# Separate PSUM tiles for a convolution's two halves, sums written straight to the gates, and later loads in a graph-network kernel

## The chip, the cores and the metric

The kernel runs on one core of a Trainium2 chip, in fp32. The time is that of the device in microseconds (us), from the start to the end of one execution. One execution was also recorded by the hardware profiler, and its trace is what the lines below come from.

A core has five engines with a queue each: PE (TensorE, the matrix products), ACT (ScalarE), DVE (VectorE), POOL (GpSimd) and SP (SyncE, which here only issues DMA transfers). Products go to PSUM, [...]a bank holds 512 fp32 values in each of 128 partitions.

## The reference, cut to what matters

One layer of a graph network over 32 graphs (batches) of 512 nodes with 256 features. `h` is the input after a layer norm and a ReLU.

```
h  = relu(layernorm(x))
hc = transpose(h)                                   # features x nodes
c  = relu(bn1(conv1x1(hc)));  c = bn2(conv17(c))    # 17 taps along the nodes
x_conv = transpose(relu(c + hc))
s  = h @ w_se.T + b_se                              # 3 values for a node
A  = exp(-|s_n - s_m|^2) * adj                      # 512 x 512
x_nmp  = A @ relu(h @ w_msg.T + b_msg)
gi = concat(x_conv, x_nmp) @ w_ih.T + b_ih;  gh = h @ w_hh.T + b_hh
r, z = sigmoid(gi_r + gh_r), sigmoid(gi_z + gh_z)
out  = x + (1 - z) * tanh(gi_n + r * gh_n) + z * h
```

The convolution with 17 taps (256 to 256 channels), the messages with their gathering, and the gates are nearly all of the products.

## The kernel before

Features lie on the 128 partitions in two halves (ND = 2), the 512 nodes of a batch along the free axis. Every batch passes through five kinds of work:

- **begin**: norm, ReLU and transpose of a batch to `hT`, which is stored to DRAM (`hd`) by POOL's queue. Three users load it back with SP: `load_row` (`hT`, for the first convolution), `load_graph` (`hTg`, for messages) and `load_gates` (`hTb`, for gates).
- **rows**: the 1x1 convolution, whose rows are the input of the long one.
- **conv**: the 17 taps as a fast convolution with 5 x 5 = 25 products. It doesn't go by batches: the nodes are cut in units of 18 rows, 29 units a batch, and the units lie in seven groups (`STARTS`). The first group has 116 units, which is four batches; the other six have some 135. A group runs its 25 products (`convolution`, L741). Each has transformed weights `w`, an operand `x` made by DVE ahead of time and, except one product of the 25 (`LONE`), a sum operand `xd`. From the second group on, a product writes both output halves into one PSUM tile `pair` of two banks (L777). Half 0 is started by four small products with `w[:, 2]`, ACT copies it into half 1, and the `xd` products are then added to both (L817 to 822). ACT then hands the finished pair over to SBUF (`both`, L620) as `n` or `z`, and DVE adds up the results of the 25 products in `y` (`summed`).
- **graph**: messages, the factors, `kernel_exp` (L878) with four products of 5 rows that run beside each other, one of which goes to the second bank of `pair` (L885) and three to banks of the pool `ps_g`; ACT takes the exponential into `at`. Then come the mask (`masked`, L897), the gathering (`gather`), and the store of `xnb` to DRAM (`nd`).
- **gates**: products with `whh` and `wih` into `ps_acc`, tanh on ACT, mixing on DVE, and the output, with `load_res` (L934) fetching the input block by block.

Between conv and gates stands `evacuate` (L679). When a group's `y` is complete, there is a list `EVAC` with an entry for each batch and half. ACT applies the batch norm to each and writes a `part`, a buffer of three, POOL stores it to DRAM (`cd`), and when all of a batch is there, `load_conv` loads it as `xconv`. `residual` (L234) adds `hTb` on DVE and takes ReLU on ACT.

The order is made by a planner that writes out every instruction beforehand. Five streams (rows, begins, graphs, conv, gates; L1308 to 1314) are Python generators with a clock of progress each; the planner takes the stream that is furthest behind and not waiting, and keeps an estimate `now` of the time on PE and of when DVE and ACT come free (`dve.free`, `act.free`). Work for DVE and ACT that isn't tied to a stream is put in between by `fill` (L1259), which runs delayed actions (`later`), evacuations and background work. An evacuation is given out only if ACT is estimated to be free soon:

```
if now < t or act.free > now + 0.3 or len(PARTS) > 2 and now < PARTS[-3]:
    return False
```

So an edit to an estimate, to a wait or to a `later` moves the order of much else. Where no stream can go on, the planner puts dummy products in at the start (`keep_warm`, L146). The helper at L127 issues all DVE and ACT work, that at L136 all products; the profile therefore names tiles and these lines.

Loads are issued by SP in the written order. A load that needs a buffer still in use makes SP wait, with all loads behind it. The weights of products are loaded from their DRAM copy by `weights_again` (L566, issued at L570), the blocks of the input by `blocks` (L929), the masks at L336 and L339, the sums at L251.

Of the kernel before, what the change touches and what calls it, by code (L numbers as in the profile page):

```python
# [13 lines left out]
P = 128  # L14
# [19 lines left out]
Q = 18  # L34
# [15 lines left out]
def kernel(  # L50
# [169 lines left out]
    def load_gates(b):  # L220
        if b >= B or b in HB:
            return
        settle_stores()
        HB[b] = late.tile([P, ND, N], F32, name="hTb", bufs=2)
        nc.sync.dma_start(HB[b], HD[b])

    def load_conv(b):

# [4 lines left out]

    def residual(b):  # L234

        if b not in XC or b in RES or now < XC_AT[b]:
            return
        dve.tensor_tensor(XC[b], XC[b], HB[b], op=ALU.add)
        RES[b] = 1e9

        def relu():
            act.activation(XC[b], XC[b], AF.Relu)
            RES[b] = act.free + LAG

        later(dve.free + 0.3, relu)
# [350 lines left out]
    def summed(g):  # L596

        nonlocal read  # L600
        y = None
        _, nh, nz, _ = sizes(g)

        def columns(name, **more):
            return cv.tile([P, NZ], F32, name=name, **more)[:, :nz]

        def add(dst, a, b, op=ALU.add):
            SUMS.append((sums_at, lambda: dve.tensor_tensor(dst, a, b, op=op)))

        def onto(f, z, op=ALU.add):  # L610
            SUMS.append((
                sums_at, lambda: dve.tensor_tensor(y[:, :, f], y[:, :, f], z, op=op)
            ))

        def more(dst, a, k, b, op=ALU.add):
            SUMS.append((
                sums_at, lambda: dve.scalar_tensor_tensor(dst, a, k, b, op0=ALU.mult, op1=op)
            ))

        def both(dst, ps):  # L620

            nonlocal bank_at, sums_at
            act.activation(dst.rearrange("p (h n) -> p h n", h=2), ps, AF.Copy)
            bank_at = sums_at = act.free + LAG

        for j1 in ORDER:
            got = yield
            sum_all(read)
            n3 = columns("n", bufs=2)
            both(n3, got)  # L630
            got = yield
            sum_all()
            settle()
            z = cv.tile([P, 3 * NZ], F32, name="z")[:, : 3 * nz].rearrange("p (e n) -> p e n", e=3)
            zends = z[:, 0:3:2, :]
            both(z[:, 0, :], got)
            add(z[:, 0, :], z[:, 0, :], n3)
            got = yield
            both(z[:, 2, :], got)
            more(z[:, 2, :], n3, 4.0, z[:, 2, :])  # L640
            got = yield
            n2 = columns("n", bufs=2)
            both(n2, got)
            got = yield
            n1 = z[:, 1, :]
            both(n1, got)
            add(n2, n1, n2, ALU.subtract)
            more(n1, n1, 2.0, n2, ALU.subtract)
            add(zends, zends, n1[:, None, :].to_broadcast([P, 2, nz]))
            more(z[:, 1, :], n3, 2.0, n2)  # L650
            read = summed_to + len(SUMS)
            if j1 == 3:

                def first(z=z):
                    nonlocal y
                    y = cv.tile([P, 9 * NZ], F32, name="y")[:, : 9 * nz].rearrange("p (e f n) -> p e f n", e=3, f=3)
                    for f in range(3):
                        later(dve.free + 0.1, lambda f=f: act.activation(
                            y[:, :, f], z, AF.Copy, scale=float(1 << f)
                        ))  # L660

                SUMS.append((None, first))
            elif j1 in (0, 4):
                onto(j1 // 2, z)
            else:
                for f in range(3):
                    onto(f, z, ALU.subtract if (f, j1) == (1, 2) else ALU.add)
        SUMS.append((sums_at, lambda: EVAC.extend(
            (dve.free + 0.3, y, g, b, o) for b in batches(g) for o in range(ND)
        )))  # L670
        yield
# [7 lines left out]
    def evacuate():  # L679

        t, y, g, b, o = EVAC[0]
        if now < t or act.free > now + 0.3 or len(PARTS) > 2 and now < PARTS[-3]:
            return False
        EVAC.pop(0)
        nu, nh, _, _ = sizes(g)
        v0 = U * b - STARTS[g]
        first, last = max(0, -v0), min(U, nu - v0)
        c = o * nu + v0 + first
        part = late.tile([P, Q * U], F32, name="part", bufs=3)[:, : Q * (last - first)]
        act.activation(  # L690
            part.rearrange("p (u h k) -> p k h u", h=2, k=9),
            y.rearrange("p e f (h n) -> p (e f) h n", h=2)[:, :, :, c : c + last - first],
            AF.Identity, bias=bn2_sh[:, o : o + 1], scale=bn2_sc[:, o : o + 1],
        )
        act.free += 0.7
# [5 lines left out]
        return True  # L701

    AHEAD = 3
    XC, XC_AT, RES, evacuated = {}, {}, {}, {}
    X2, X_AT, XD = [], [], {}
    at_product = 0
# [34 lines left out]
    def convolution():  # L741
# [28 lines left out]
        for g in range(NG):  # L770
# [3 lines left out]
            if g == 1:  # L774
                first_ctx.close()
                cps = ctx.enter_context(tc.tile_pool(name="cps2", bufs=1, space=PSUM))
                pair = cps.tile([P, 2, N], F32, name="ps_c")  # L777
                matmul(pair[:, 1, :NH], ident, h1[:, :NH], start=True, stop=True)
                wide = True
            for n in range(25):  # L780
                at_product = m = 25 * g + n
                if n == 6:
                    yield lambda: not EVAC
                while 25 <= len(WS) < min(m + 3, 25 * NG):
                    weights_again(len(WS))
                if m == 24:
                    yield lambda: len(WS) >= 25
# [23 lines left out]
                    product(ps[:, nh:], *[(0, *d1)][n == LONE :], (1, *d2))  # L811
                else:
                    in_product = True
                    ps = pair[:, :, :nh]
                    if n == LONE:
                        for k in range(2):
                            product(ps[:, k, :], (1, x2[:, 1 - k, :], k), clear=(True, False))  # L817
                    else:
                        product(ps[:, 0, :], (2, x2[:, 1, :], 0), clear=(True, False))
                        act.activation(ps[:, 1, :], ps[:, 0, :], AF.Copy)  # L820
                        yield act.free + LAG
                        for k in range(2):
                            product(ps[:, k, :], (k, XD[m][:, k, :], 0), clear=(False, False))
                        del XD[m]
                WS[m] = X2[m] = None
                done = ps if g > 0 else ps.rearrange("p (h n) -> p h n", h=2)
                if g > 0:
                    later(now + 0.3, hand)
                at_product = m + 1
                yield now  # L830
                if g > 0:
                    yield lambda: done is None
# [45 lines left out]
    def kernel_exp(at):  # L878
# [3 lines left out]
        if not wide:  # L882
            extra = acc.tile([P, N], F32, name="ps_acc")
        else:
            extra = pair[:, 1, :]  # L885
        pss = [extra, bank(), bank(), bank()]
        for c in range(NT):
            k = slice(32 * c, 32 * c + 5)
# [8 lines left out]
    def masked(b, at, c):  # L897
# [4 lines left out]
        if b < TURNED:  # L902
# [2 lines left out]
                turn(ps[:, k * P : (k + 1) * P], m[:, k * P : (k + 1) * P])  # L905
            part = at[:, :, c * P : (c + 1) * P]
            dve.tensor_tensor(part, ps.rearrange("p (k n) -> p k n", k=NT), part, op=ALU.mult)
            gr.ask(1)
            return
        dve.transpose(gr.right, gr.masks.pop((b, c)))  # L910
        later(dve.free + 1.5, lambda: gr.ask(1))
        dve.tensor_tensor(at[:, c, :], gr.right, at[:, c, :], op=ALU.mult)

    def gather(b, msg, at, d):
# [26 lines left out]
    def begin(b):  # L941
# [4 lines left out]
        if b >= TURNED:  # L946
# [17 lines left out]
            nc.gpsimd.dma_start(HD[b], HT[b])  # L964
            begun, turning = b + 1, False
            if b + 2 < B:
                load(b + 2)
            return
        if b == 2:
            yield lambda: told > 0  # L970
# [20 lines left out]
    def graph(b):  # L991
# [12 lines left out]
            yield now  # L1004
        told = b + 1
        factors()
        load_graph(b + 1)
        yield dve.free + LAG
        factors_t()
        yield act.free + LAG  # L1010
        settle_stores()
# [12 lines left out]
        yield dve.free + LAG  # L1024
        for d in range(ND):
            gather(b, msg, at, d)
            yield now

    def gates(b):

        load_gates(b)
        load_sums(b, 0)
        load_sums(b, 1)
        if b == 0:
# [7 lines left out]
        def products(ps, o, g, ks, then=None, of=None, clear=True):  # L1042
# [4 lines left out]
            for k in ks:  # L1047
# [7 lines left out]
                if k == ks[-1] and then is not None:  # L1055
                    then()
                if k == 2 and o == ND - 1 and g == 2:
                    load_sums(b + 1, 0)
                    load_sums(b + 1, 1)
                yield now  # L1060

        def mix_next(r, ps_n, z, o, s):
# [40 lines left out]
        def store(y, o, s):  # L1103
# [6 lines left out]
                )  # L1110
            if s.stop == N:
                del XR[b, o]
                later(now + 12.0, lambda: load_res(b + 1, o))

        for o in range(ND):
            r = z = None
# [44 lines left out]
            if o == 0:  # L1161
                ps_h = acc.tile([P, N], F32, name="ps_acc")
                yield from products(ps_h, o, 2, (0,), lambda: hidden_half(ps_h))
                if b not in XC:
                    yield lambda: b in evacuated
                    yield evacuated[b]
                    load_conv(b)
                if b not in RES:
                    yield XC_AT[b]
                    residual(b)  # L1170
                yield lambda: RES[b] < 1e9
                yield RES[b]
                x_in.extend([XC[b][:, i, :] for i in range(ND)] + [XN[b, d] for d in range(ND)])
            yield from products(ps_r, o, 0, (1, 2), reset, (0, 2))
# [20 lines left out]
            yield from products(ps_z, o, 1, (0, 1, 2), update)  # L1195
            if o == 0:
                load_gates(b + 1)
                load_conv(b + 1)
            else:
                residual(b + 1)  # L1200
            if not is_last(o):
                reset_hidden()
                yield hidden_at
# [55 lines left out]
    def fill():  # L1259
        while LATER and LATER[0][0] <= now:  # L1260
            LATER.pop(0)[1]()
        if EVAC:
            evacuate()
        while dve.free < now + 1.5 and background():
            pass

# [33 lines left out]
    def all_gates():  # L1300
# [9 lines left out]
        "begins": (all_begins(), 1.05 * PER, -0.15),  # L1310
        "graphs": (all_graphs(), 11.5 * PER, -0.5),
        "conv": (convolution(), 80.0, 0.0),
        "gates": (all_gates(), 31.25 * PER, 1.6),
    }
    clock = {name: at for name, (_, _, at) in streams.items()}
    ready = {name: 0.0 for name in streams}
# [114 lines left out]
```

## Time and profile before

| | us |
|---|---|
| median of three runs | 2119.8 (2118.39 to 2119.88) |
| the profiled execution | 2118.86 |
| its span | 2116.8 |
| PE busy | 2060.8 (97%) |
| DVE busy | 1367.1 (65%) |
| ACT busy | 815.4 (39%) |
| POOL busy | 337.7 (16%) |
| PE's mean granted clock | 0.987 |

The span is what the trace covers. "Busy" is the union of an engine's instructions. The waits of PE say for each kind of instruction how long PE was idle ahead of it, how many times, the longest one, and which instruction or transfer ended the wait. The granted clock is the share of full speed that the hardware gave PE. Some durations of single instructions or transfers that the steps use:

| what | us |
|---|---|
| ACT, `at` from PSUM (128x512) | 0.604 |
| ACT, copy in `ps_c` (128x270) | 0.385 |
| ACT, hand-over to `z` (128x540) | 0.619 |
| ACT, `part` of 522 columns, strided | 1.334 |
| ACT, `y` from `z`, three in a row | 1.546 each |
| transfer `w` from DRAM, to landing | 5.2 |
| transfers hd to DRAM / `hT` back | 5.8 / 4.7 |
| transfers cd to DRAM / `xconv` back | 3.7 / 6.5 |
| transfers `res` / `xnb` | 2.4 / 3.0 |

### The profile page before, as it was taken

Reading aid. Unit: us, or ns where it says so; the run is one execution under the profiler, and the core shown is the slowest. Engines: PE = TensorE matmul, PEld = TensorE weight load, DVE = VectorE, ACT = ScalarE, POOL = GpSimd, SP = SyncE. Lnnn points to the kernel's source line nnn. Section 1 sums busy time; section 2 is a strip of 40 time slices with the busy share of each in tenths; the row PEclk is TensorE's granted clock in tenths of the full one; section 3 lists DMA queues with packets and bytes.
Section 4 is the critical chain, followed back from the end, with each engine's and each line's share of the span. In section 5 each row is a group of like instructions: output and inputs, shape, how many; then the busy total and the mean of one; then the engine's idle time right before and its main releaser. Section 6 shows DMA issues by size and latency. Waiting matters only on the chain.

```text
span 2116.8 us, 25837 instructions
## 1 busy us (share of the span) xinstructions
PE 2060.8 (97%) x8714; PEld 1264.5 (60%) x8714; DVE 1367.1 (65%) x2441; ACT 815.4 (39%) x1431; POOL 337.7 (16%) x582
## 2 busy tenths in 40 slices
PE   9999889999999999999999999989999999999998
PEld 6887656665566645666555665556665656654444
DVE  6888568857677457777486863576674857663323
ACT  5544453333533344433454324433234442224121
POOL 2011121211201022111121110121111110112111
PEclk9999989999999999999999999999999999999999
DMA  7445777776777767767776776676667566525342
GB/s 279 167 174 185 254 224 205 201 227 170 189 211 199 228 152 212 200 149 222 191 184 196 195 205 176 168 177 184 193 176 212 140 176 171 152 84 141 85 95 40
DMA packets 546467, 380.44 MB, mean 180 GB/s; under 512 B 456608, under 2 KB 473536, under 8 KB 545696
## 3 DMA queue, kind: packets, MB, share of 16 engines
q1 hardware_dynamic: 513136, 279.81, 49.5%
q0 software_dynamic: 28512, 85.75, 13.3%
q10 hardware_dynamic: 4688, 13.24, 1.6%
q8 instruction: 69, 1.13, 0.2%
q14 instruction: 62, 0.51, 0.1%
HBM read 279.60 MB, written 99.09 MB: 179 GB/s over the span
## 4 chain that ended last, share of the span: by engine, by line
PE 86%; issue 6%; DVE 3%; DMA 2%; ACT 1%; POOL 1%; SPq 1%; POOLq 0%; DVEq 0%; ACTq 0%
PE ps_acc L136 43%; PE ps_c L136 22%; PE ps_g L136 18%; PE ps_g L141 1%; PE ps_c L889 1%; ACT at L127 1%; DMA hT<-hd 0%; PE ps_acc L146 0%; POOL out_dram L1107 0%; DMA cd<-part 0%; DVE z L127 0%; DMA w<-wd 0%; DMA m_sb<-in_adj_dram 0%; SPq L929 0%; DMA hd<-hT 0%
## 5 line engine op out<-in xcount | busy, mean ns | idle before, releaser
L136 PE MATMUL ps_acc<-xconv,wih 128*128 128x512 f32 (+1 forms) x772 | 365.7, 596 | 1.9 <-ACT xconv L127 1.9
L136 PE MATMUL ps_acc<-xnb,wih 128*128 128x512 f32 (+1 forms) x772 | 360.5, 592 | 0.0
L136 PE MATMUL ps_acc<-hTb,whh 128*128 128x512 f32 (+1 forms) x772 | 357.5, 592 | 0.0
L136 PEld LDWEIGHTS ps_c<-xd,w 128*128 128x128 f32 x2304 | 288.9, 191 | 66.9 <-issue 58.3
L136 PEld LDWEIGHTS ps_c<-x,w 128*128 128x128 f32 x2032 | 260.3, 194 | 107.8 <-issue 57.2
L136 PE MATMUL ps_c<-x,w 128*128 128x135 f32 (+2 forms) x2032 | 269.8, 282 | 29.7 <-ACT at L127 15.1
L136 PE MATMUL ps_c<-xd,w 128*128 128x135 f32 (+1 forms) x2304 | 291.2, 279 | 1.0 <-ACT ps_c L127 1.0
L1107 POOL DMA_DIRECT2D out_dram<-res x252 | 164.1, 658 | 619.9 <-DVE res L127 559.8
L136 PEld LDWEIGHTS ps_acc<-xconv,wih 128*128 128x128 f32 x772 | 142.6, 192 | 148.4 <-issue 144.0
L136 PE MATMUL ps_g<-at,msg 128*128 128x512 f32 x512 | 229.7, 599 | 0.6 <-DVE at L127 0.5
L136 PEld LDWEIGHTS ps_acc<-xnb,wih 128*128 128x128 f32 x772 | 141.9, 191 | 141.8 <-issue 139.5
L136 PEld LDWEIGHTS ps_acc<-hTb,whh 128*128 128x128 f32 x772 | 141.1, 190 | 141.1 <-issue 138.2
L127 DVE TENSOR_TENSOR msg<-ps_g,bmsg 128x256 f32<-128x256 f32 x128 | 53.8, 421 | 186.2 <-PE ps_g L136 185.8
L136 PEld LDWEIGHTS ps_g<-at,msg 128*128 128x128 f32 x512 | 96.3, 192 | 112.3 <-issue 107.9
L127 DVE TENSOR_TENSOR o_sb<-hTb,r 128x512 f32<-128x512 f32 x63 | 43.4, 688 | 151.2 <-ACT r L127 151.2
L127 DVE SCALAR_TENSOR_TENSOR x<-x,x 128x544 f32<-128x544 f32 (+5 forms) x161 | 137.7, 856 | 3.1
L127 DVE TENSOR_TENSOR xd<-x 128x544 f32<-128x544 f32 (+1 forms) x144 | 102.8, 718 | 47.4 <-PE ps_c L136 47.0
L136 PE MATMUL ps_g<-hT,w 128*128 128x512 f32 (+8 forms) x296 | 120.7, 558 | 9.8 <-DMA hT<-hd 9.8
L127 DVE TENSOR_TENSOR x<-x 128x272 f32<-128x272 f32 (+5 forms) x280 | 127.1, 497 | 0.4
L127 ACT ACTIVATE ps_c<-ps_c 128x270 f32<-128x270 f32 (+1 forms) x144 | 55.6, 386 | 182.9 <-PE ps_c L136 182.6
L136 PE MATMUL ps_g<-wmsg,hTg 128*128 128x259 f32 x496 | 123.7, 381 | 0.0
L127 ACT ACTIVATE h<-ps_g,bn_shift,bn_scale 128x252 f32<-128x252 f32 (+8 forms) x212 | 86.7, 484 | 85.3 <-PE ps_g L136 85.2
(124 smaller groups left out, 2278.9 us busy)
## 6 DMA issues: line engine op xcount, KB each, us to landing
w<-wd SPq DMA_DIRECT2D x120, 768.0 KB, 5.2
m_sb<-in_adj_dram SPq DMA_DIRECT2D x384, 64.0 KB, 3.1
hT<-hd SPq DMA_DIRECT2D x33, 512.0 KB, 4.7
hd<-hT POOLq DMA_DIRECT2D x32, 512.0 KB, 5.8
hTb<-hd SPq DMA_DIRECT2D x32, 512.0 KB, 5.3
xnb<-nd SPq DMA_DIRECT2D x64, 256.0 KB, 3.0
xconv<-cd SPq DMA_DIRECT2D x32, 512.0 KB, 6.5
res<-in_x_dram SPq DMA_DIRECT2D x256, 64.0 KB, 2.4
```

The costliest lines, as they stand in the source:

```text
L127: getattr(self.engine, name)(*tiles, **more)
L136: nc.tensor.matmul(ps, lhsT, rhs, **more)
L141: nc.tensor.transpose(ps, a, ident)
L889: nc.tensor.matmul(pss[c], gr.left[k, :], gr.right[k, :], start=True, stop=True, tile_position=(32 * c, 0),)
L1107: queue.dma_start(OB[b][:, s.start // 32 : s.stop // 32, o * P + 32 * g : o * P + 32 * g + 32], y[at, s].rearrange("i (k j) -> i k j", j=32),)
```

## The change

Four edits in one.

1. `pair` becomes a list of two tiles, `ps_c0` and `ps_c1`, one bank each. `both` hands each over with an ACT instruction of its own. The extra bank of `kernel_exp` is the second tile.
2. For the first two batches of the first group, `evacuate` writes the sums with two ACT instructions a half (504 and 8 columns) straight into `xconv`; there is no `part`, no store and no load. The other evacuations stay, and all are given out while ACT is estimated to be busy for at most 0.9 us more (0.3 before).
3. Loads are put later in the order: weights two products ahead instead of three, and asked for within or after the product; masks after the mask product or the gathering; the next batch's input, sums and graph operand some 2 us later or after a yield; the next input block at the store of the one before.
4. Loading `xconv` and taking the residual are polled in `fill` for the batch in the gates and the one after, instead of standing in `gates`. The gates' clock starts at 1.8 instead of 1.6.

```diff
 def residual(b):
-    if b not in XC or b in RES or now < XC_AT[b]:
+    if b not in XC or b in RES or now < max(XC_AT.get(b, 1e9), HB_AT.get(b, 1e9)):
         return
...
 def both(dst, ps):
     nonlocal bank_at, sums_at
-    act.activation(dst.rearrange("p (h n) -> p h n", h=2), ps, AF.Copy)
-    bank_at = sums_at = act.free + LAG
+    if len(ps) == 1:
+        act.activation(dst, ps[0], AF.Copy)
+    else:
+        for k, half in enumerate(ps):
+            n = half.shape[-1]
+            act.activation(dst[:, k * n : (k + 1) * n], half, AF.Copy)
+            if k == 0:
+                bank_at = act.free + LAG
+    sums_at = act.free + LAG
...
 def evacuate():
     t, y, g, b, o = EVAC[0]
-    if now < t or act.free > now + 0.3 or len(PARTS) > 2 and now < PARTS[-3]:
+    if now < t or act.free > now + 0.9 or len(PARTS) > 2 and now < PARTS[-3]:
         return False
...
+    ys = y.rearrange("p e f (h n) -> p (e f) h n", h=2)
+    if g == 0 and b < 2:
+        if o == 0:
+            XC[b] = late.tile([P, ND, N], F32, name="xconv", bufs=2)
+        full = N // Q
+        for dst, src in (
+            (XC[b][:, o, : Q * full].rearrange("p (u h k) -> p k h u", h=2, k=9), ys[:, :, :, c : c + full]),
+            (XC[b][:, o, Q * full :], ys[:, : N - Q * full, 0, c + full]),
+        ):
+            act.activation(
+                dst, src, AF.Identity, bias=bn2_sh[:, o : o + 1], scale=bn2_sc[:, o : o + 1]
+            )
+        if o == ND - 1:
+            evacuated[b] = XC_AT[b] = act.free + 0.7 + LAG
+        return True
     part = late.tile([P, Q * U], F32, name="part", bufs=3)[:, : Q * (last - first)]
...
-                pair = cps.tile([P, 2, N], F32, name="ps_c")
-                matmul(pair[:, 1, :NH], ident, h1[:, :NH], start=True, stop=True)
+                pair = [cps.tile([P, N], F32, name=f"ps_c{k}") for k in range(2)]
+                matmul(pair[1][:, :NH], ident, h1[:, :NH], start=True, stop=True)
...
-                while 25 <= len(WS) < min(m + 3, 25 * NG):
+                while 25 <= len(WS) < min(m + 2, 25 * NG):
                     weights_again(len(WS))
...
-                        product(ps[:, 0, :], (2, x2[:, 1, :], 0), clear=(True, False))
-                        act.activation(ps[:, 1, :], ps[:, 0, :], AF.Copy)
+                        product(ps[0], (2, x2[:, 1, :], 0), clear=(True, False))
+                        act.activation(ps[1], ps[0], AF.Copy)
                         yield act.free + LAG
+                        if 25 <= len(WS) == m + 2 < 25 * NG:
+                            weights_again(m + 2)
...
                 at_product = m + 1
+                if 25 <= len(WS) == m + 2 < 25 * NG:
+                    weights_again(m + 2)
...
-            extra = pair[:, 1, :]
+            extra = pair[1]
...
-            gr.ask(1)
+            later(now + 1.0, lambda: gr.ask(1))
             return
         dve.transpose(gr.right, gr.masks.pop((b, c)))
-        later(dve.free + 1.5, lambda: gr.ask(1))
+        if c > 0:
+            gr.ask(1)
...
-                load(b + 2)
+                later(now + 2.0, lambda: load(b + 2))
...
         factors()
-        load_graph(b + 1)
         yield dve.free + LAG
+        load_graph(b + 1)
...
             gather(b, msg, at, d)
+            if d == 0 and b >= TURNED:
+                gr.ask(1)
...
-                    load_sums(b + 1, 0)
-                    load_sums(b + 1, 1)
+                    for d in range(ND):
+                        later(now + 2.0, lambda d=d: load_sums(b + 1, d))
...
-                later(now + 12.0, lambda: load_res(b + 1, o))
+                load_res(b + o, 1 - o)
...
-                if b not in XC:
-                    yield lambda: b in evacuated
-                    yield evacuated[b]
-                    load_conv(b)
-                if b not in RES:
-                    yield XC_AT[b]
-                    residual(b)
-                yield lambda: RES[b] < 1e9
+                yield lambda: RES.get(b, 1e9) < 1e9
                 yield RES[b]
...
                 load_gates(b + 1)
-                load_conv(b + 1)
-            else:
-                residual(b + 1)
...
 def fill():
...
+    for b in (gating, gating + 1):
+        if b in HB:
+            load_conv(b)
+            if dve.free < now + 1.5:
+                residual(b)
...
-        "gates": (all_gates(), 31.25 * PER, 1.6),
+        "gates": (all_gates(), 31.25 * PER, 1.8),
```

More of the change, by code (lines that the diff above doesn't have):

```diff
@@ L225, in load_gates @@
         nc.sync.dma_start(HB[b], HD[b])
+        HB_AT[b] = now + 8.0
     def load_conv(b):
@@ L691, in evacuate @@
             part.rearrange("p (u h k) -> p k h u", h=2, k=9),
-            y.rearrange("p e f (h n) -> p (e f) h n", h=2)[:, :, :, c : c + last - first],
+            ys[:, :, :, c : c + last - first],
             AF.Identity, bias=bn2_sh[:, o : o + 1], scale=bn2_sc[:, o : o + 1],
@@ L703 @@
     AHEAD = 3
+    HB_AT, gating = {}, 0
     XC, XC_AT, RES, evacuated = {}, {}, {}, {}
@@ L813, in convolution @@
                     in_product = True
-                    ps = pair[:, :, :nh]
+                    ps = [bank_[:, :nh] for bank_ in pair]
                     if n == LONE:
                         for k in range(2):
-                            product(ps[:, k, :], (1, x2[:, 1 - k, :], k), clear=(True, False))
+                            product(ps[k], (1, x2[:, 1 - k, :], k), clear=(True, False))
                     else:
-                        product(ps[:, 0, :], (2, x2[:, 1, :], 0), clear=(True, False))
-                        act.activation(ps[:, 1, :], ps[:, 0, :], AF.Copy)
+                        product(ps[0], (2, x2[:, 1, :], 0), clear=(True, False))
+                        act.activation(ps[1], ps[0], AF.Copy)
                         yield act.free + LAG
+                        if 25 <= len(WS) == m + 2 < 25 * NG:
+                            weights_again(m + 2)
                         for k in range(2):
-                            product(ps[:, k, :], (k, XD[m][:, k, :], 0), clear=(False, False))
+                            product(ps[k], (k, XD[m][:, k, :], 0), clear=(False, False))
                         del XD[m]
                 WS[m] = X2[m] = None
-                done = ps if g > 0 else ps.rearrange("p (h n) -> p h n", h=2)
+                done = ps if g > 0 else [ps]
                 if g > 0:
@@ L1006, in graph @@
         factors()
+        yield dve.free + LAG
         load_graph(b + 1)
-        yield dve.free + LAG
         factors_t()
@@ L1026, in graph @@
             gather(b, msg, at, d)
+            if d == 0 and b >= TURNED:
+                gr.ask(1)
             yield now
     def gates(b):
+        nonlocal gating
         load_gates(b)
+        gating = b
         load_sums(b, 0)
```

## The prediction

> **What bounds the kernel now.** I read the page first: the busy shares, then the chain that ended last.
>
> ```profile
> PE 2060.8 (97%) x8714; PEld 1264.5 (60%) x8714; DVE 1367.1 (65%) x2441; ACT 815.4 (39%) x1431; POOL 337.7 (16%) x582
> ...
> PE 86%; issue 6%; DVE 3%; DMA 2%; ACT 1%; POOL 1%; SPq 1%; POOLq 0%; DVEq 0%; ACTq 0%
> ```
>
> TensorE sets the time; all other engines have slack. A change that leaves its products alone can win only its idle time (2116.8 - 2060.8 = 56 us) and the time lost to a lowered clock. The second view, the waits of PE, names the idle time (columns: total us, times, longest us):
>
> ```profile
> PE ps_c L136 <- ACT at L127: 15.1, 18, 3.2
> PE ps_g L136 <- DMA hT<-hd: 9.8, 3, 5.8
> PE ps_c L136 <- ACT n L127: 8.9, 3, 3.7
> PE ps_c L136 <- DVE x L127: 3.4, 1, 3.4
> PE ps_c L136 <- ACT z L127: 2.3, 1, 2.3
> PE ps_acc L136 <- ACT xconv L127: 1.9, 1, 1.9
> PE ps_acc L146 <- POOL mhalf L272: 1.8, 1, 1.8
> PE ps_c L889 <- ACT z L127: 1.5, 1, 1.5
> ```
>
> Third, busy time in windows (after the length: busy us of PE, PEld, DVE, ACT, POOL; then granted clock, DMA share, GB/s), to see where it lies:
>
> ```profile
> 106.00:212.00 106.00, 106.00 (x706) 85.72 (x704) 90.23 (x177) 50.98 (x100) 12.49 (x23) 1.00 0.54 180
> 212.00:318.00 106.00, 91.22 (x432) 62.86 (x431) 65.77 (x127) 50.39 (x86) 17.16 (x28) 0.90 0.74 237
> 1272.00:1378.00 106.00, 102.14 (x330) 53.67 (x329) 48.50 (x84) 43.53 (x80) 16.92 (x27) 0.98 0.65 169
> 1378.00:1484.00 106.00, 96.95 (x399) 60.07 (x398) 73.22 (x137) 41.63 (x69) 18.55 (x28) 0.94 0.67 181
> ```
>
> Most stretches have PE busy over 103 of 106 us at a clock of 0.98 to 1.00. Two are bad: the start of the second group (idle 14.8, clock 0.90) and the one around 1388 (idle 9.1, clock 0.94). Fourth, PE's timeline at those places (start, length, operation; in brackets the idle time before it and its releaser):
>
> ```profile
> 235.77 1.43 PE L136 MATMUL ps_c<-x,w 128*128 128x136 f32 x8 [3.36 <-DVE x L127]
> 279.81 1.20 PE L136 MATMUL ps_c<-x,w 128*128 128x136 f32 x8 [2.81 <-ACT n L127]
> 298.67 3.99 PE L136 MATMUL ps_c<-x,w 128*128 128x136 f32 x16 [3.68 <-ACT n L127]
> 312.42 1.20 PE L136 MATMUL ps_c<-x,w 128*128 128x136 f32 x8 [0.67 <-ACT at L127]
> ```
>
> The last stands for 16 like it: right after the exponentials' four small products, the next convolution product waits 0.67 us for ACT to read one of them. The same gap is 1.17 at 1143 and 3.22 at 1460.
>
> **What the Trainium skill says.** "TensorE: Matmul & The Clock Gate", Part 1, says that an idle window lowers TensorE's clock until it has been busy again for about one more. The trace agrees: 10 us slices that follow a gap of over about 1 us show 0.83 (230:240, 280:290, 1310:1320), which is 10 x 0.17 = 1.7 us lost a gap. The slices below 0.97 lose some 25 us together. "PSUM — Partial Sum Buffer", "PSUM bank collisions raise a hardware error", asks for guards by bank; two tiles in two banks are guarded apart, one tile over both is not: that is the 0.67. Its "Engine vs sequencer instructions" calls ScalarE's queue strictly first in, first out: an evacuation put in it delays a hand-over behind it, as under (b). "DMA: Bandwidth & Descriptors", "Two DMAs through the same engine are not ordered", has a dependent transfer wait for the first's completion: hT<-hd cannot start before hd<-hT has landed (median 5.8 us), and SP's waits show that one, 41.8 us in 7 waits at L211.
>
> **(a) Two tiles.** 18 gaps, 15.1 us. In the order of the changed kernel the first product after exp writes ps_c0 only, while exp's extra output lies in ps_c1: it has no wait on ACT. What is late next is its copy into ps_c1, behind ACT's reads: exp 1.2 us, read 0.6, product 0.9, copy 0.4, so about 3.4 us after exp begins. Until the xd products need it, 1.2 + 0.9 + some 3.4 us of gate products stand on PE at nearly all places: 5.5 > 3.4, hidden. Without those gate products about 1.3 us a place would be lost. One place is left: near PE work 816 a product without a third term writes ps_c1 at once, and three y<-z writes (4.5 us together) stand ahead of `at` in ACT, as they did at 1460: 2.5 lost. The lower clock after 1143 goes too, 1.7. Sum: -15.1 + 2.5 - 1.7 = -14.3. Ends: -17 if that place is free as well, -6 if half of the places lack filler.
> Splitting a hand-over: 150 of them, each 2 x 385 ns instead of 619, 0.15 us more, 23 us of ACT. ACT is idle 61% of the time; it hides, save where a hand-over is waited for (c. 20 places, 3 us, put under (e)).
>
> **(b) Start of the second group.** I added trace durations along PE's order in both kernels ("PE work"). Between the bank change (230.40) and the first xconv product (302.45) lie 48 us of work, done in 72.05: 24 lost, 14 idle and 10 to the clock. Part of it is the way of the first sums: four parts to DRAM and two loads back (part 1.33, cd<-part 3.7, xconv<-cd 6.5) before the first residual; ACT's timeline shows one that stood 5.65 us until a cd store freed a buffer, with the n hand-over behind it for which PE waits the 2.81 above:
>
> ```profile
> 277.96 1.35 ACT L127 ACTIVATE part<-y,bn_shift,bn_scale 128x522 f32<-128x522 f32 x1 [5.65 <-DMA cd<-part]
> 279.11 0.66 ACT L127 ACTIVATE n<-ps_c 128x544 f32<-128x544 f32 x1
> ```
>
> For batches 0 and 1 all this goes: 4 stores, 2 loads. ACT writes xconv itself, in two instructions a half: no row has them; the strided part of 504 columns took 1.30 and conv1's 8 columns 0.36, so 1.7 against 1.33. By the scalar page ("ScalarE: Activation LUTs", "What ACT_TABLE_LOAD costs") a contiguous one with two pointers would be 280 + 93 + 0.833 x 504 = 793 ns, the lower bound; 2.6 (twice the strided one) the upper; I take 1.7, 6.8 for all. The first xconv product now comes at 234.6 of PE work instead of 257.5, and the group's first product gets 16.5 us of other work ahead of it, which covers the 3.36 for DVE's x. But the four evacuations stand in ACT ahead of the n hand-over whose bank exp wants (about 3.2 idle) and of `at`, which holds banks (2.4 + 1.0), so about 9 us idle (with some 2.4 of smaller gaps) and 4.5 for the clock stay: 24 - 13.5 = 10.5 gained. Ends 4 (all collisions come again) and 18.
>
> **(c) hT loads.** The 3.86 at 1314 and 5.83 at 1388 are batches 26 and 27, stored and loaded just before use: store 5.8, load 4.7 to 5.2, so some 11.5 us, with 0 and 1.7 us of PE work between store and use. In the changed order these are 10.5 and 8.1: 1 and 4 left (the store stands behind other POOL work), of 9.7. Gain 4.7, plus a little for the clock: -5. Ends 0 and -12.
>
> **(d) Residual asked earlier.** The xconv wait of 1.94 at 1716 and its clock: -3.6. Ends 0 and -5. Elsewhere it was hidden.
>
> **Loads asked for later** cost nothing by themselves: SP's waits lose 473.1 (res) and 289.9 us (weights), but no engine waits for these loads. Cover: res and xnb have over 8 us of PE work between store and use against 2.4 and 3.0 us. A weight load comes one product nearer; products are 1600/150 = 10.7 us apart against 5.2 landing. Where two are under 5 us apart, it would be late by up to 2 us. Ends 0 and +6.
>
> **(e) What is added.** Ten more dummy products (L146, 142 for 132 in the order, 0.15 each): 1.5. Evacuations may now be queued behind 0.9 us of ACT work instead of 0.3, and 0.7 less is booked for the direct ones, so hand-overs meet them: in the order I see four places (PE work 540, 792, 1042, 1612) with a part or two right ahead of a hand-over, 1.1 us each beyond cover, 4.5, and 3 for clocks. Sum +9. Ends +2 and +16. POOL issues four stores fewer, SP two loads fewer; DVE is unchanged in number (2444), and its moved residual has DVE's 35% idle.
>
> **Sum.** -14.3 - 10.5 - 5 - 3.6 + 9 = -24.4. Against the profiled execution (2118.86: span 2116.8 and 2.06 around it) 2094.5; the median is 0.9 higher: 2095.
>
> **Rivals.** *Only the tiles gain:* an order written out anew makes new meetings for those removed; (c) and (d) nothing, (b) 4: -14.3 - 4 + 9 = -9.3, 2110. For it: the gaps move with the order, as 1460 shows. Against: stores and loads are truly gone. *All closes:* -17 - 18 - 12 - 3.6 + 1.5 = -49, 2071. For it: 61% of ACT is free. Against: the y<-z burst is in the new order. *Slower, by ACT's queue:* a part (1.33) admitted 0.9 late ahead of a hand-over makes a product wait 2.2, and 1.7 of clock: 3.9. The gains are 33.4, so from 9 such meetings of some 70 parts on it is slower; at 12, +13, 2133. Before has 4 of this kind (n 3, z 1); that speaks against. *It doesn't do what it says:* the 0.67 stays because the copy is waited for; then -24.4 + 12 = 2107.
>
> **Numbers.** Likeliest case 0.58, its own range 2080 to 2106; only tiles 0.16; wait stays 0.06; all closes 0.08; slower 0.12. The range leaves out half of "all closes" and the slower case: 2071 to 2119. A measurement tells 0.2%, 4.2 us, from no change: faster 0.82, same 0.06, slower 0.12.
>
> **What would show it.** Right: no wait of ps_c on ACT `at` but one or two; the slices 230 to 310 at 0.95 or more in most; no xconv<-cd for two batches (x30); hT<-hd waits under 6 us. Wrong: ps_c waits on ACT (xconv, part, n, z) above 20 us; waits on w<-wd; a slice under 0.9 in new places, as that costs more than its gap.

## The result, and the profile after

The changed kernel takes 2085.2 us (median of four runs, 2083.4 to 2089.1) against 2119.8 before (2118.4 to 2121.0). The ratio is 0.9839, with a 95% interval of 0.9822 to 0.9856: 34.7 us faster, where 25 were forecast and the range reached to 2071. The execution that was profiled took 2089.1, the slowest of the four; its span is 2087.2, so the two traces differ by 29.6 us, and what follows accounts for these.

The page of the changed kernel, busy shares and the chain that ended last:

```profile
PE 2053.2 (98%) x8724; PEld 1260.0 (60%) x8724; DVE 1364.5 (65%) x2441; ACT 827.7 (40%) x1585; POOL 337.4 (16%) x578
...
PE 93%; DVE 3%; ACT 2%; DMA 1%; issue 1%; POOL 0%; SPq 0%; ACTq 0%; DVEq 0%
```

PE's idle time fell from 56.0 to 34.0 us, and its busy time by 7.6 although it has ten instructions more. That second part is about what the clock explains: its mean rose from 0.987 to 0.990, some 6 to 7 us over the span. The waits of PE after (total us, times, longest):

```profile
PE ps_c L136 <- ACT z L127: 4.7, 2, 4.4
PE ps_c L136 <- ACT at L127: 3.2, 1, 3.2
PE ps_c L136 <- ACT n L127: 2.9, 4, 1.2
PE ps_g L136 <- ACT h L127: 2.8, 1, 2.8
```

The 18 waits on `at` (15.1 us) are one of 3.2; the hT waits (9.8) and the xconv wait (1.9) are not in the list any more. Instead there is one of 2.8 on `h`, the 1x1 convolution's output, and one of 4.4 on `z`. The two bad stretches, in windows after the change (columns as before):

```profile
212.00:318.00 106.00, 101.02 (x471) 66.30 (x470) 73.80 (x139) 58.70 (x111) 17.70 (x27) 0.97 0.73 229
1378.00:1484.00 106.00, 106.00 (x486) 67.58 (x485) 75.97 (x142) 40.87 (x80) 15.48 (x22) 1.00 0.71 197
```

PE went from 91.2 to 101.0 us busy in the first and from 97.0 to 106.0 in the second, and the clock from 0.90 to 0.97 and from 0.94 to 1.00. Busy time by clock, the work that got done, rose from 82.1 to 98.0 in the first: 16 us gained there alone. (The clock is printed to a hundredth, so such a product is good to about half a us.)

The three longest gaps that are left in PE's timeline:

```profile
721.82 5.40 PE L136 MATMUL ps_g<-hT,w 128*128 128x512 f32 x8 [2.78 <-ACT h L127]
830.76 1.85 PE L136 MATMUL ps_c<-x,w 128*128 128x135 f32 x8 [3.23 <-ACT at L127]
1563.21 2.17 PE L136 MATMUL ps_c<-x,w 128*128 128x135 f32 x8 [4.37 <-ACT z L127]
```

The middle one is the collision that the prediction placed near PE work 816 with 2.5 us: `at` stands in ACT behind three y<-z writes (4.44 us) and two writes of x_sb. The other two were not foreseen; what is late there shows in DVE's waits, of the kernel before and of the changed one:

```profile
DVE hT L127 <- DMA x_sb<-xd: 56.8, 17, 9.7
...
DVE w L127 <- DMA w<-wd: 26.0, 7, 7.8
...
DVE hT L127 <- PE ps_c L136: 13.2, 1, 13.2
...
DVE hT L127 <- PE ps_g L136: 5.8, 2, 3.7
```

```profile
DVE hT L127 <- PE ps_g L136: 25.6, 4, 9.2
DVE hT L127 <- DMA x_sb<-xd: 6.8, 3, 3.0
DVE w L127 <- DMA w<-wd: 3.0, 1, 3.0
```

Before, DVE stood 83 us in its queue for two kinds of load. After, it stands 10 us for them. Its transposes into `hT` also wait for PE, which still reads the buffer: 19 us before, 26 after. That kind of wait is not new, but before PE had no gap behind it; after, it has two. At 717 one of them held DVE for 9.20 us. Behind it came the residual, ACT's ReLU of `xconv` behind that, and behind this the `h` for which PE waits the 2.78. At 1559 another held DVE for 4.36 us, with the addition to `y` behind it for which `z` waits. This is where some of the gain was given back: 7.2 us of idle time, and the clock after it. One of the prediction's signs of being wrong came as well: slices under 0.9 in new places (460, 720, 830, 970 and 1560).

### The profile page after: what moved, and what is told of

Read it like the earlier page. It is cut to its first block, busy times and chain, and to the rows that moved or that the text cites. A ratio compares the mean times of both kernels' runs of the same rounds, so it can differ in the third digit from the quotient of the medians.

```text
span 2087.2 us, 25989 instructions
## 1 busy us (share of the span) xinstructions
PE 2053.2 (98%) x8724; PEld 1260.0 (60%) x8724; DVE 1364.5 (65%) x2441; ACT 827.7 (40%) x1585; POOL 337.4 (16%) x578
## 4 chain that ended last, share of the span: by engine, by line
PE 93%; DVE 3%; ACT 2%; DMA 1%; issue 1%; POOL 0%; SPq 0%; ACTq 0%; DVEq 0%
PE ps_acc L136 47%; PE ps_c L136 22%; PE ps_g L136 21%; PE ps_g L141 1%; PE ps_c L917 1%; DVE z L127 1%; DMA xconv<-cd 0%; PE ps_acc L146 0%; DVE st L127 0%; ACT h L127 0%; PE ps_g L917 0%; DVE x L127 0%; ACT y L127 0%; ACT x_sb L127 0%; DVE at L127 0%
## 5 line engine op out<-in xcount | busy, mean ns | idle before, releaser
L127 ACT ACTIVATE z<-ps_acc,brz 128x512 f32<-128x512 f32 x64 | 43.9, 686 | 188.8 <-PE ps_acc L136 188.8
```

The costliest lines, as they stand in the source:

```text
L127: getattr(self.engine, name)(*tiles, **more)
```

## The experiments

All times are compared with the runs of the kernel before on the same chip, as ratios; the changed kernel's is 0.9839. Differences between versions are taken from the ratios, not from the times. A hundredth of ratio is 21 us.

**One tile again, in the order of the changed kernel; two tiles, in the order of before.** The planner knows nothing of tiles, so the order can be held fixed and only the waits change.

```diff
-                pair = [cps.tile([P, N], F32, name=f"ps_c{k}") for k in range(2)]
+                whole = cps.tile([P, 2, N], F32, name="ps_c")
+                pair = [whole[:, k, :] for k in range(2)]
```

> The changed kernel with its two PSUM tiles made one tile again (both halves are slices of it). Every engine's instructions stand in the same order as in the changed kernel, so only what a product has to wait for differs. By the prediction's part (a) the waits of 0.67 us after the exponentials' products come back at some 18 to 26 places: 12 to 18 us of waits on ACT `at`, and the kernel is 13 to 20 us slower than the changed one, about 2100. The rival (the wait is only handed on to the copy, tiles do nothing) expects 2 us or less, 2085 to 2087.

Measured: 2101.9 us, ratio 0.9914 (0.9896 to 0.9931), 16 us slower than the changed kernel. In the other direction, `both` in the kernel before issues two copies and books one:

```diff
-            act.activation(dst.rearrange("p (h n) -> p h n", h=2), ps, AF.Copy)
...
+                act.free = max(act.free, now) + act.fixed + act.each * elements(dst)
+                for k, half in enumerate(ps):
+                    n = half.shape[-1]
+                    nc.scalar.activation(dst[:, k * n : (k + 1) * n], half, AF.Copy)
```

> The kernel before with two PSUM tiles and the hand-over split in two, and the planner's accounts left as they were, so that the order is that of before (ACT has 150 more instructions in it). Part (a) expects 15.1 us of waits on ACT `at` to fall to about 3 (the place at 1460 stays), 12 us of idle time and 1.7 of clock: about 2106. All other gaps (hT<-hd 9.8, ACT n 8.9) should stay. The rival that split hand-overs cost time expects the waits of ps_c on ACT n and z to grow from 11 to over 15 us and the time to stay above 2112.

Measured: 2101.9 us, 0.9919 (0.9900 to 0.9938), 17 us faster than before. The waits of PE with one tile in the changed order, and with two in the order of before:

```profile
PE ps_c L136 <- ACT at L127: 15.7, 16, 4.3
```

```profile
PE ps_g L136 <- DMA hT<-hd: 11.1, 3, 5.4
...
PE ps_c L136 <- ACT at L127: 2.2, 1, 2.2
```

The waits on `at` come and go with the tiles (3.2 to 15.7 and 15.1 to 2.2), and the hT waits stay. The rivals fall: the wait is not handed on to the copy (1.3 us against 1.0), and the hand-overs' waits stayed near 11.5 us. As the first edit leaves the split hand-over in place, it is the tiles and not the split that do it. The time moved by 3 to 4 us more than these waits; in the second run PE is busy 6.6 us less than in the kernel before (2054.2), which is clock, while the first run's trace has no such difference.

**The first sums through DRAM in the changed kernel, and written directly in the kernel before.** The first edit turns the condition off; the second adds the direct branch to `evacuate` in the kernel before, with the gates' wait for it, and nothing else:

```diff
-        if g == 0 and b < 2:
+        if False:
```

> The changed kernel with the first two batches' sums sent through DRAM like the others. Part (b) expects the start of the second group to be some 10 us slower, idle time and clock together: about 2095, with the stretch 212 to 318 at a PE busy of 93 to 97 us and a clock near 0.93. The rival (that stretch is gained by the order, not by the way of the sums) expects the stretch to stay at 100 or more and the time within 4 us of 2085.

> The kernel before with only the first two batches' sums written straight to the gates. Part (b) expects about 10 us less, 2110, with the stretch 212 to 318 at 97 us of PE busy or more. The rival expects no change of that stretch (91 us) and a time within 5 us of 2120, since the new order only deals the gaps out anew.

Measured: 2086.7 us, 0.9850 (0.9830 to 0.9870), and 2129.9 us, 1.0057 (1.0039 to 1.0076). So the changed kernel did not lose by going without the direct writing, and the kernel before lost 12 us by having it alone. The stretch itself, first in the changed kernel without it, then in the kernel before with it:

```profile
212.00:318.00 106.00, 95.18 (x459) 62.91 (x459) 73.35 (x137) 55.74 (x102) 19.70 (x31) 0.98 0.74 241
```

```profile
212.00:318.00 106.00, 92.25 (x446) 63.22 (x445) 69.22 (x133) 52.20 (x91) 15.71 (x24) 0.94 0.73 227
```

Busy time by clock: 98.0 falls to 93.3 without it, and 82.1 rises to 86.7 with it. The direct writing is worth about 4.6 us there, both ways, not 10.5; the rest comes from the other edits or the new order. The total does not show it, as the order was dealt out anew further on: without it, the gaps at 721 and 830 are gone, and one of 4.84 stands at 515. With it alone in the kernel before, a gap of 10 us appeared far away. The lines are PE's, DVE's and SP's timeline of that run:

```profile
837.38 2.93 PE L136 MATMUL ps_acc<-xconv,wih 128*128 128x512 f32 x3 [10.01 <-ACT xconv L127]
```

```profile
835.01 1.23 DVE L127 TENSOR_TENSOR xconv<-xconv,hTb 128x1024 f32<-128x1024 f32 x1 [9.93 <-DMA xconv<-cd]
```

```profile
829.51 0.38 SPq L231 DMA_DIRECT2D xconv<-cd  x1
```

The kernel before asks for the next batch's `xconv` at one fixed place in the gates, right behind `hTb`. If the batch isn't evacuated by then, the load waits for the next batch's gates. Here `hTb` went out at 781.5 with no `xconv` behind it, since the parts were still being stored (781 to 793); the load followed at 829.5, and its 5.5 us, the residual and the ReLU stood open on PE. In the kernel before itself the two go out together, at 789.4 and 789.9. Two later runs with the old gates (below) met the same gap, 10.1 and 11.0 us.

**Evacuations at 0.3.**

```diff
-        if now < t or act.free > now + 0.9 or ...
+        if now < t or act.free > now + 0.3 or ...
```

> The changed kernel with evacuations given out only at 0.3 us of estimated ACT work, as before, instead of 0.9. Part (e) priced the allowance at 7.5 us lost (4.5 of waits, 3 of clock), so it expects about 2078. The rival that the allowance lets the evacuations, and so all that waits for their end, come earlier expects it slower, 2088 or more. The profile of the changed kernel shows few waits on ACT hand-overs with a part ahead of them, which speaks for 2085 give or take 4.

Measured: 2076.1 us, 0.9810 (0.9795 to 0.9824), some 6 us faster than the changed kernel, with intervals that just touch. The size fits part (e), the mechanism doesn't. In the changed kernel ACT's timeline has the bursts where they were predicted (540, 800, 1062, 1640), for instance

```profile
539.82 1.35 ACT L127 ACTIVATE part<-y,bn_shift,bn_scale 128x522 f32<-128x522 f32 x1 [3.01 <-DMA cd<-part]
...
1061.96 1.34 ACT L127 ACTIVATE part<-y,bn_shift,bn_scale 128x522 f32<-128x522 f32 x1 [2.24 <-DMA cd<-part]
```

but PE has no gap of 0.7 us at any of these places. ACT's waits for a part's buffer did fall from 7.5 to 0.4 us with 0.3; the gaps of PE that vanished are others (2.78 at 721, 4.37 at 1563, and 1.80 at 255). A part of the difference is no wait at all: the gap of 1.00 us at 462 is still there, but the clock after it is not lowered this time (last section).

**All loads where they were before**, with weights three products ahead, and so on for masks, input, sums, graph operand and input blocks.

> The changed kernel with all loads asked for where they were before (weights three products ahead, input, masks, sums and graph operand at once, input blocks 12 us after the store). The prediction priced the later loads at nothing: 2085 give or take 4, with SP waiting again some 400 us or more for the input blocks. The rival that the later loads keep SP's queue free for hT, and so remove the hT waits, expects 5 us or more of hT<-hd waits to come back and 2092 or more.

Measured: 2101.8 us, 0.9924 (0.9908 to 0.9941), 18 us slower. The prediction priced this at nothing. The way in which it costs can be read at one place, from SP to DVE to PE:

```profile
365.73 1.92 SPq L953 DMA_DIRECT2D res<-in_x_dram  x4
367.75 0.43 SPq L571 DMA_DIRECT2D w<-wd  x1
```

```profile
371.79 0.69 DVE L127 TENSOR_TENSOR w<-w 128x512 f32<-128x512 f32 x1 [9.29 <-DMA w<-wd]
```

```profile
379.51 3.78 PE L136 MATMUL ps_acc<-xconv,wih 128*128 128x512 f32 x4 [5.95 <-DVE ps_acc L127]
```

The load of an input block had been put in the order long before its buffer was free; SP stood 14.5 us for an output store. The weights queued behind it came late, DVE's sum `w[:, 2]` waited 9.29 us for them, and the scaling of `ps_acc` that PE needs was behind it in DVE's queue. SP's waits on out_dram<-res are 443 us in this run, 58 in the changed kernel. No engine waits for the input blocks, but two queues further on one waits for what stands behind them. DVE's waits for the two kinds of load in this run:

```profile
DVE w L127 <- DMA w<-wd: 22.7, 6, 9.3
DVE hT L127 <- DMA x_sb<-xd: 14.1, 6, 6.8
```

Those for weights are nearly back, those of the transposes are not. As the rival foresaw, PE's hT waits return too, with 5.8 us. In the traces PE is idle 10.5 us more than in the changed kernel, and these and the 5.95 would make that up; but other gaps went and came with the order (3.37 at 237 came, 2.78 at 721 and 3.23 at 831 went), so the 18 us are a price of all the loads in this order, not of the one chain.

**One line of the loads.** With all loads put back, the start of the second group looked like that of before, gap by gap. By the order, a single line does that: in the kernel before, `load_graph(1)` is called while batch 1 has not begun, so nothing is issued, and the graph stream loads it at its own start and is held for the planner's 9 us. Moved after the yield, the call finds batch 1 begun. In the traces of the two kernels the load goes out at 28.9 us after the change and at 44.1 before it, and the messages of batch 1 run at 52.9 and at 62.3.

```diff
         factors()
-        load_graph(b + 1)
         yield dve.free + LAG
+        load_graph(b + 1)
```

> The kernel before with one line moved: the next batch's graph operand is asked for after the yield that follows the factors. In the kernel before it is asked for while batch 1 has not begun, is not given out, and the graph stream then loads it at its own start and is held for the planner's 9 us; after the yield, batch 1 has begun. The new theory (this line sets the start of the second group, for its messages come some 10 us earlier) expects the stretch 212 to 318 to have PE busy for 98 us or more instead of 91, and about 2107. The rival (the direct writing of the sums set it, or several edits together) expects 91 to 93 us there and a time within 5 us of 2118.

> The changed kernel with that one line moved back, all other edits kept. The new theory expects what the run with all loads put back showed: 10 us or more lost, about 2097, with the gaps of before at the start of the second group (3.4 on DVE x at 236, 1.5 ahead of the small products near 260, 2.5 or more near 275). The rival (other later loads did it) expects 2085 give or take 4 and no DVE x wait at 236.

Measured: 2128.4 us, 1.0061 (1.0044 to 1.0078), and 2081.4 us, 0.9835 (0.9820 to 0.9849). The theory falls as a price of the whole: alone the line makes the kernel slower, and the changed kernel does as well without it. In the stretch it is a part: 82.1 us of work rise to 86.4 with it alone (busy 91.87, clock 0.94), and 98.0 fall to 88.8 without it (96.54, 0.92), with the gap on DVE x back (3.06 at 237.7). But its run alone has the missed `xconv` load (10.07 at 837), and the run without it has no gaps at 721 and 830. Against the run with all loads put back, this one has only that line back, and is 0.0089 or 19 us faster: so what the later loads gain as a whole lies in the other ones.

**The line and the two tiles, in the kernel before.** PE's order is that of the line alone.

> The kernel before with two edits only: that line, and two PSUM tiles with the planner's accounts left alone (PE's order is that of the run with the line alone). If these two carry the change, their gains add: 17 for the tiles and what the line alone gives, about 2091 if it gives 10. If the direct writing, the polling or the other loads are needed for the gain, it stays above 2098.

Measured: 2112.3 us, 0.9980 (0.9969 to 0.9992). The tiles give 0.0081 once more, 17 us; the missed `xconv` load is 11.0 us here. Two edits don't carry the change.

**The residual at fixed places, in the changed kernel.** The lines of the gates are put back and the loop in `fill` is taken out.

> The changed kernel with the residual taken and xconv loaded at fixed places in the gates, as before. Part (d) expects 3.6 us more, 2089, as a wait of ps_acc on ACT xconv of 2 us or more in one place. The rival that the polling also takes work out of the planner's stalls (gates held up where xconv was not there yet) expects 8 us or more, 2093.

Measured: 2084.8 us, 0.9858 (0.9841 to 0.9874): no difference outside the intervals. In this order the fixed place is not missed. The wait on `xconv` does not come back (0.3 us at most), so it is not shown that the polling took it away; the order may have.

**The gates' clock, alone and with the evacuations at 0.3.** The first adds no instruction and takes none away.

```diff
-        "gates": (all_gates(), 31.25 * PER, 1.8),
+        "gates": (all_gates(), 31.25 * PER, 1.6),
```

> The changed kernel with the gates' clock at 1.6 as before: no wait and no instruction is added or taken away, only the order of the streams is another. It measures how much the order alone deals out: if the parts carry the gain, 2085 give or take 4; if the order does, it may differ by 8 us or more, with gaps at other places of the same kinds.

> The changed kernel with the gates' clock at 1.6 and evacuations at 0.3. Each alone gave 9 and 12 us. If the 0.9 allowance costs by itself (part (e)), the two add to about 2064. If each only dealt the order out anew, it lands anywhere from 2066 to 2090, and the floor of PE's own work, near 2050 with the start and the end, keeps it from going much lower.

Measured: 2073.0 us, 0.9791 (0.9776 to 0.9806), and 2061.0 us, 0.9739 (0.9724 to 0.9753). The order alone moves 10 us. Both together are the fastest version, 2.6% below the kernel before and 1.0% below the changed one. (By the ratios the two alone gave 6 and 10 us, not the 9 and 12 of the expectation, which compared times.) Its page:

```profile
PE 2041.4 (99%) x8724; PEld 1252.9 (61%) x8724; DVE 1365.6 (66%) x2441; ACT 829.0 (40%) x1585; POOL 337.1 (16%) x578
```

No gap of PE over 1.9 us is left; the mean clock is 0.997, and PE's busy time is 11.8 us below that of the changed kernel for the same products. The 0.3 gave 6 us in the first order and 11 in this one (0.9791 to 0.9739), so two orders agree that it helps, the first of them barely. By which way is not settled: in the first of them PE's gaps at 721 and 1563 went, and the second order had neither to begin with. In both orders the clock from 460 to 470 is 0.66 without the 0.3 and 1.00 with it, which is 3.4 us each time; one trace of each can't tell this from chance.

## Why the prediction was right, and where not

The sign and the range were right, and the likeliest case too (its own range began at 2080). By its steps:

| step | predicted us | what the runs showed |
|---|---|---|
| (a) two tiles | -14.3 | -16, -17 and -17 in three orders |
| (b) start of the second group | -10.5 | -16 in the stretch; direct writing 4.6 of it |
| (c) hT loads | -5 | -9.8 of idle time |
| (d) residual earlier | -3.6 | -1.9 of idle time in the trace; 0.2% at most when undone |
| later loads | 0 | 18 us slower when undone |
| (e) what is added | +9 | no PE gap at the four places; new ones elsewhere |

(a) held in its mechanism and nearly in size. The place left over was where it was said to be, at 3.2 instead of 2.5. The clock was counted once, after 1143; the runs moved 2 to 3 us more than the sum, and one of the two traces with a fixed order shows more of it as clock.

(b) was short, and credited to the wrong edit. The direct pair was priced well (504 columns took 1.312 and 8 columns 0.366 us; predicted 1.7 for both), and the two waits that it would leave, 3.2 and 3.4, were 1.80 and 1.39. What failed is the step from the order to the cause: the whole 10.5 was credited to leaving out the way through DRAM, which is worth 4.6 there. With the line of `load_graph` (4.3 alone, 9.2 when taken out of the whole) and the tiles (2.9 alone), it is one of several contributions of like size; they add up to less than the 16.

(c) expected 5 of 9.8 to stay; none did. The step took 11.5 us of store and load against 10.5 and 8.1 of PE work, with the store "behind other POOL work". It left out what comes ahead of the store. Before, at the first of the two places,

```profile
1302.41 0.71 DVE L127 STREAM_TRANSPOSE hT<-x_sb 128x512 f32<-128x512 f32 x1 [9.71 <-DMA x_sb<-xd]
```

and store (1305.4), load (1311.1) and product (1314.7) follow upon it. In the changed kernel DVE's waits for x_sb<-xd fell from 56.8 to 6.8 us. The changed kernel and all its variants with the new loads have hT waits of 2.1 us or less, all kernels built on the one before 9.3 to 12.7; with the old loads in the changed kernel it is 5.8, at other places. Which edit freed the transposes stays open. The later loads alone did not: with the old ones DVE stands 14.1 us for x_sb<-xd, far from 56.8.

"Loads asked for later cost nothing by themselves" is the step that failed outright. It looked at who waits for each of these loads, and found nobody. It did not ask what stands behind them in SP's queue: weights and batch blocks, for which DVE waited 83 us, and behind DVE's head of queue the scaling that PE needs. (With the old loads the waits for weights came back, those for the blocks mostly not.) That no engine waits for the weights was wrong even as read: DVE's waits before the change show w<-wd with 26.0 us, and only PE's and SP's lists had been read.

(e) had the places right and the cost wrong: four bursts, no gap. In its stead PE now stood behind DVE's transposes that wait for an hT buffer, 7.2 us at two places. The rivals: that only the tiles gain (2110) is refused by the result. The slower rival, by ACT's queue, has no support; but slower did happen, twice, by another mechanism, a load missed at a fixed place in the gates, when one edit was made alone.

How far the sum was luck: undone one at a time, the tiles cost 16 us and the later loads 18, nearly the 34.7 together, and the direct writing and the polling cost nothing outside the intervals. The loads were priced at nothing, and (b), (c) and (d), priced at 19, were partly their work or the order's. The total was met, but not by the parts that were named for it; and as the order alone moves 10 us, the two prices need not add up.

## What to carry to other kernels

A load that nobody waits for still costs what stands behind it in its queue: read the waits of every engine, not those of the bound one alone, and follow a late transfer through the queues. Where a planner writes the order, hold the order fixed to price one edit (the tiles gave 16 to 17 us in each of three orders), and measure what the order alone deals out (10 us here) before any difference of that size is credited to an edit. A place fixed for a load can be missed when anything else moves: it cost some 2 us or less in two orders here and some 10 us in two others.

## What the runs showed of the hardware

The clock that PE loses after a gap does not go by the gap's length. The prediction's rule, a lower clock after gaps of over about 1 us, fails in the kernel before already: after the gap of 2.28 us at 449 the next 10 us ran at 1.00, and 750 to 760, with a gap of 0.30 us, ran at 0.83. The products show that this loss is real. Four equal ones took 3.40 us there and 1.88 elsewhere:

```profile
751.58 3.40 PE L136 MATMUL ps_acc<-xconv,wih 128*128 128x512 f32 x4
777.42 1.88 PE L136 MATMUL ps_acc<-xconv,wih 128*128 128x512 f32 x4
```

One and the same gap can cost or not. This one stands in the changed kernel and, with the same products around it, in the run with the evacuations at 0.3:

```profile
462.60 2.07 PE L917 MATMUL ps_g<-right,left 5*128 5x512 f32 x2 [1.00 <-ACT h L127]
460.02 1.12 PE L917 MATMUL ps_g<-right,left 5*128 5x512 f32 x2 [1.00 <-ACT h L127]
```

From 460 to 470 the clock was 0.66 in the first and 1.00 in the second: 3.4 us, of a gap of 1.00. In finer windows of the changed kernel the clock is 0.50 while it is lowered, for 3.4 us (at 722 and 831) or 6.8 us (at 462 and 1562). So a gap cost nothing, 1.7 us or up to 3.4 us, and the prediction's 1.7 us a gap is an average at best. Each trace shows one execution; what decides between these cases is not shown.
